# Two-head attention stage of a decoder: transposing the byte weights on TensorE instead of by DMA, with a rearranged schedule around it

## The chip, the core and the metric

The kernel runs on one core of a Trainium2 chip. A core has five engines with queues of their own: TensorE (PE, matrix multiplication into PSUM, with its weight loads as PEld), VectorE (DVE), ScalarE (ACT), GpSimd (POOL) and SyncE (SP, which here only issues DMAs). [...] Each engine works its queue in order: an instruction that waits holds up everything behind it. The metric is the device time of one execution in microseconds; lower is better.

## The reference

The program is a two-layer decoder over 2048 tokens of width 256. In each layer come an attention block, a cross-attention to a context of 2048 rows, and an MLP (a mixture of experts in the second layer), each followed by a layer norm. The change lies in layer 0, in the cross-attention and the MLP behind it:

```
q = fq_sym((x @ Wq + bq) / sqrt(16))          # 16 heads of 16, rounded to 8 bits per row
k = fq_sym(kv[..., 0]); v = fq_sym(kv[..., 1], axis=keys)
attn = softmax(q @ k.T)                       # 2048 queries x 2048 keys per head
attn = fq_unsigned(attn, axis=-1)             # rounded to 0..255 of the row's maximum
x = layernorm(x + (attn @ v) @ Wp + bp)
x = layernorm(x + (silu(gate) * up) @ w_down) # gate, up = x @ w_gate_up, inner width 1024
```

Since the weights are rounded to 256 steps of the row's maximum, the kernel computes exp(s - max + ln 255) straight into bytes.

## The kernel before

Cross-attention and MLP of layer 0 run as one "joint stage". The 2048 queries are 16 tiles of 128, taken as 8 pairs; a pair is 16 **steps**, (pair gp, head pair i, tile u), 128 steps in all. A step handles 2 heads x 128 queries x 2048 keys, and is issued in two **periods** (part 0 and 1), each over 1024 keys.

For step n, in order of the pipeline:

- `scores` (line 767): four bf16 matmuls a period on TensorE, 64 rows deep, so that head 0 and head 1 lie in different halves of the array. They write two PSUM tiles s, one a head, 4 KB per partition (two of the eight banks). Three such tiles exist; the rest of PSUM is one bank for the contexts (o) and one for everything else (misc).
- `scaled` (774): VectorE multiplies by the query's scale out of PSUM into e, and takes the row maximum on the way; two a period, one for each head. The second half's maximum includes that of the first.
- `exponent` (786): ScalarE makes the bias from the maxima at the end of the step.
- `weights8` (795): one step later, ScalarE writes exp as bytes a (128 queries x 2048 keys), head 0 in period 0, head 1 in period 1. Straight after it SP issues a DMA transpose (803) of a, seen as 128 x 1024 16-bit words, into at.
- `spread` (807): two steps after the scores, GpSimd takes the bytes of at apart (two to a word) and casts them to bf16 as aT, keys on the partitions.
- `context` (817): three to five steps after the scores, TensorE multiplies aT by the values, 16 matmuls for each pair of steps: 6 in period 1 of even steps, 5 in each period of odd steps.

The keys' order in the value tile (`values_by_key`, before the stage) matches the order in which the bytes come apart.

Between these, `pair_work` hands out pieces of other work by the step's number r in its pair and the period: queries for the next pair, whose quantised rows are transposed by DMA (`query_cols`, 612), division, output projection and layer norm of the pair before, and the MLP. An MLP unit is one of 8 slices of the inner width, in two halves `ffn_half` (gate and up, line 889, two f32 matmuls each), then tanh, copy and an affine step on ScalarE (907, 908, 911) and two products on GpSimd (914, 915). The units ran one per step at r = 8 to 15, and the down projection (924) at r = 1 to 3 of the next pair. TensorE's f32 matmuls each show as two records in the trace; its f32 transposes as one.

The order on all engines is written by hand (`manual_schedule`): what the loop emits is what the queues hold, and `later`/`due` put a piece off to a named period and place ("DVE", "ACT first", "ACT", "POOL", "SP" and so on). After the last step, up to 9 more steps drain the pipeline, and the last pair's MLP follows.

Of the kernel before, what the change touches and what calls it, by code (L numbers as in the profile page):

```python
# [20 lines left out]
U8 = mybir.dt.uint8  # L21
# [27 lines left out]
def decoder(ctx: ExitStack, tc: tile.TileContext, w: dict, out: bass.AP):  # L49
# [79 lines left out]

    pair_mv = {}  # L130

# [6 lines left out]

    def norm_pair(q):
        mv = pair_mv.pop(q)  # L140
        rstd = stat.tile([P, 2], F32, tag="np_rstd", name="np_rstd")
        nc.gpsimd.tensor_scalar(rstd, mv[:, :, 1], 1.0, 1e-5, ALU.mult, ALU.add)
        nc.gpsimd.tensor_tensor(rstd, rstd, mhalf, ALU.pow)
        shift = stat.tile([P, 2], F32, tag="np_shift", name="np_shift")
        nc.gpsimd.tensor_scalar(shift, mv[:, :, 0], -1.0, 0.0, ALU.mult, ALU.add)
        nc.gpsimd.tensor_tensor(shift, shift, rstd, ALU.mult)
        for i in range(2):
            x = xs[2 * q + i]
            nc.gpsimd.tensor_scalar(x, x, rstd[:, i : i + 1], shift[:, i : i + 1], ALU.mult, ALU.add)
# [420 lines left out]
    with ExitStack() as ph:  # L570
# [39 lines left out]

        def query_cols(t):
            nc.sync.dma_start_transpose(out=qT[t % 4].bitcast(U16), in_=rows3.rearrange("p h d -> p (h d)").bitcast(U16))

        qs = {}
        with tc.tile_pool(name="l0x_1", bufs=1) as p1, tc.tile_pool(name="l0x_p0", bufs=2, space=PSUM) as ps0:
# [35 lines left out]
            def values_by_key(t4):  # L651
                pt = ps0.tile([P, 4, 2, P], BF16, tag="pt3", name="ptv")
                for i in range(4):
                    for c in range(2):
                        at = t4 * G + (i // 2) * 2 * P
                        keys = vqT[:, c, at : at + 2 * P].rearrange("p (w j) -> p j w", j=2)
                        nc.tensor.transpose(pt[:, i, c, :], keys[:, i % 2, :], ident16)
                nc.scalar.copy(vq[:, 4 * t4 : 4 * t4 + 4, :].rearrange("p t (c d) -> p t c d", c=2), pt)
# [49 lines left out]
            for n in range(NB + 4):  # L708

                if n < NG:  # L710
                    values_of(n)
                if n < NB:
                    key_scale(n)
                for stage, f in ((1, key_steps), (2, key_round), (3, key_parts), (4, key_cols)):
                    if 0 <= n - stage < NB:
                        f(n - stage)
                if n == 3:
                    nc.vector.memset(rows3, 0.0)
                if n in (5, 8):
                    t = n // 8  # L720
                    a = query_max(t, query_proj(t, ps0, "pk"), p1)
                    query_scale(t)
                    query_round(a, query_inverse(t))
                if n in (7, 10):
                    query_cols(n // 10)
                if n == 4:
                    value_scale()
                if n in (6, 9, 12, 15):
                    quantise_values(n // 3 - 2)
                if n in (7, 10, 13, 16):  # L730
                    values_by_key(n // 3 - 2)
# [27 lines left out]
        def scores(gp, i, u, half, st):  # L759

            t = 2 * gp + u
            s = [ps.tile([P, 2, G], F32, tag="s", name="s", bufs=3) for _ in range(2)]
            for c in range(2):
# [24 lines left out]
        def weights8(gp, i, u, hh, st):  # L788
# [4 lines left out]

            a = wk.tile([P, 2 * G], U16, tag="a", name="a", bufs=3)
            nc.scalar.activation(  # L795
# [5 lines left out]
            )  # L801
            at = wk.tile([P, 8, P], U16, tag="at", name="at", bufs=4)
            nc.sync.dma_start_transpose(out=at, in_=a)
            st["at"].append(at)

        def spread(u, hh, st, aT):
            nc.gpsimd.tensor_copy(  # L807
                aT[:, :, hh, u * P : (u + 1) * P].rearrange("p (b j) q -> p b j q", j=2),
                st["at"][hh].bitcast(U8).rearrange("p b (q j) -> p b j q", j=2),
            )  # L810
# [70 lines left out]
        def ffn_gate(q, i, n, tag="misc"):  # L881

            if n == 0:
                pp = ps.tile([P, 2, G] if tag == "s" else [P, 2, 2 * P], F32, tag=tag, name="gu", bufs=3 if tag == "s" else 1)
                ffn_ps[q] = pp[:, 0].rearrange("p (n c) -> p n c", n=2) if tag == "s" else pp
# [23 lines left out]

        def ffn_sigmoid(th):  # L910
            nc.scalar.activation(th, th, AF.Copy, bias=0.5, scale=0.5)

# [4 lines left out]
        def ffn_down_psum(tag="misc"):  # L917
            pp = ps.tile([P, 2, G] if tag == "s" else [P, G], F32, tag=tag, name="pd", bufs=3 if tag == "s" else 1)
            return (pp[:, 0] if tag == "s" else pp).rearrange("p (u d) -> p u d", u=2)
# [29 lines left out]
        def query(t, at):  # L949
# [13 lines left out]
            later(at + 4, "POOL", lambda: query_round(box["a"], box["r"]))  # L963
            later(at + 5, "SP", query_cols, t)

# [7 lines left out]
        def put_out(gp, js, at):  # L973
# [7 lines left out]
            if 7 in js:  # L981
                later(at + 1, "POOL", norm_pair, gp)

        def ffn_half(q, i, n, at):
# [3 lines left out]
            if n == 1:  # L988
                th, gu = ffn_tiles(q, i)
                later(at, "ACT", ffn_out, q, th, gu)  # L990
                later(at + 1, "ACT", ffn_sigmoid, th)
                later(at + 2, "POOL", ffn_mult, q, i, th, gu, nc.gpsimd)
# [3 lines left out]
        def ffn_put_out(q, js, at, tag="misc"):  # L996
# [7 lines left out]
            if 2 * NI - 1 in js:  # L1004
                later(at + 1, "POOL", norm_pair, q)

# [6 lines left out]
        def by_dim(gp, u):  # L1013
            rbs[gp, u] = sums_by_dim(gp, u)

        def pair_work(n, end):

            gp, r = n // 16, n % 16
            at = 2 * n + end
            turn = (r, end)  # L1020
            if gp < LAST and turn in ((0, 0), (4, 0)):
                query(2 * gp + 2 + r // 4, at)

            if gp > 0:
                if turn == (4, 1):
                    divided(gp - 1, at)
                elif turn in ((5, 1), (6, 0), (6, 1)):
                    j = 3 * (2 * r + end - 11)
                    put_out(gp - 1, range(j, min(j + 3, 8)), at)
                elif turn == (7, 1):  # L1030
                    transposed(gp - 1, at)
                if turn in ((6, 0), (6, 1), (7, 0)):
                    ffn_load(2 * r + end - 12)
                if r >= 8 and not end:
                    ffn_half(gp - 1, r - 8, 0, at)

            if gp > 1:
                if (1, 0) <= turn <= (3, 1):
                    j = (0, 3, 6, 8, 11, 14, 16)[2 * r + end - 2 :]
                    ffn_put_out(gp - 2, range(j[0], j[1]), at)  # L1040
                elif turn == (5, 0):
                    transposed(gp - 2, at)

        def tail_work(n, end):
# [3 lines left out]
            turn = (r, end)  # L1048
            if turn in ((1, 0), (1, 1), (4, 0)):
                j = {(1, 0): (0, 4), (1, 1): (4, 8), (4, 0): (8, 16)}[turn]  # L1050
                ffn_put_out(LAST - 1, range(*j), at, "s")
# [11 lines left out]
        turns = {(7, 0): (0, 3), (7, 1): (3, 6), (8, 0): (6, 8), (8, 1): (8, 11), (9, 0): (11, 13), (9, 1): (13, 16)}  # L1063
        ordered = [getattr(mybir.EngineType, nm) for nm in ("PE", "DVE", "Activation", "Pool", "SP")]
        with tc.manual_schedule(engines=set(ordered)):
            for n in range(len(steps) + 9):
                now = steps[n] if n < len(steps) else None
                if now is not None:
                    if n % 16 == 0:
                        group(n // 16)  # L1070
                    if n < NB:
# [3 lines left out]
                        "mx": stat.tile([P, 2, 2], F32, tag="smx", name="smx"),  # L1075
                        "at": [],
                    }
                for part in range(2):
                    at = 2 * n + part
                    if now is not None:  # L1080
                        s = scores(*now, part, states[n])
                        scaled(*now, part, 0, states[n], s)
                        due(at, "DVE")
                        scaled(*now, part, 1, states[n], s)
                    else:
                        due(at, "DVE")
                    gp, r = n // 16, n % 16
                    if part == 1 and 0 < gp <= LAST and r >= 8:
                        ffn_half(gp - 1, r - 8, 1, at)
                    for hh in range(2):  # L1090
# [28 lines left out]
                    if 0 <= n - 2 < len(steps):  # L1119
                        gp, i, u = steps[n - 2]  # L1120
                        if part == 0 and u == 0:
                            aTs[gp, i] = wk.tile([P, NB, 2, 2 * P], BF16, tag="aT", name="aT")
                        spread(u, part, states[n - 2], aTs[gp, i])
                    due(at, "POOL")
                    if now is not None and part == 1:
                        exponent(states[n])
                    due(at, "DVE last")
                    due(at, "SP")
                    if (n, part) == (len(steps), 1):
# [7 lines left out]
                if n == len(steps) + 3:  # L1137
                    ffn_load_all()
                states.pop(n - 2, None)
            assert not put_off, put_off  # L1140

            for i in range(NI):
# [3 lines left out]
                ffn_out(LAST, th, gu)  # L1146
                ffn_sigmoid(th)
                ffn_mult(LAST, i, th, gu, nc.vector)
            exp_tables()
            for u in range(2):  # L1150
                ffn_put_out(LAST, range(NI * u, NI * u + NI), 0, "s")
                due(1, "DVE")
            due(1, "POOL")

    early_stage.close()
# [496 lines left out]
```

## Time and profile before

| | us |
|---|---|
| median of 3 runs | 2724.48 (2720.74 to 2729.77) |
| the profiled execution | 2727.17 |
| its span | 2725.2 |
| first to last start of the scaling, line 774 (the joint stage) | 880.4 to 1613.8 |
| byte casts on GpSimd, line 807, first to last start | 892.6 to 1626.4 |
| one DMA transpose of at on SP's queue, median | 1.23 |

| busy share of the span | PE | PEld | DVE | ACT | POOL |
|---|---|---|---|---|---|
| whole program | 92% | 55% | 70% | 54% | 45% |

In rows of groups, the fields are: line, engine, operation, written and read tiles, shapes and count; then total busy us and mean ns of one; then the engine's idle time just before the group and what ended it. In rows of the timeline: start us, duration, engine, line, operation, tiles, and in brackets the idle time before and its releaser. A row of waits gives the waiting engine and tile, whom it waited for, total us, times, longest. Durations are those of records, and on VectorE and ScalarE one record's end overlaps the next one's start by about 0.1 us, so the distance from start to start is the cost in a row of work. The whole-program shares mix stages with different limits; only the stretch from 880 to 1620 us concerns this change.

### The profile page before, as it was taken

The page shows a single profiled execution, that of the slowest core. Times are in us where ns is not written, and L with a number is a line of the kernel's source. Part 1 is how long each engine was busy: PE and PEld are TensorE (multiplying, and loading weights), DVE is VectorE, ACT ScalarE, POOL GpSimd, SP SyncE. Part 2 cuts the span into 40 slices and gives each one's busy share as a digit, 9 for nine tenths or more (in the row PEclk, how much of TensorE's full clock was granted, in tenths as well). Part 3 has the DMA queues.
Part 4 walks back from the last instruction along what each step waited for, and adds up shares of the span by engine and source line. Part 5 has one row for each costly group of instructions (what it writes and reads, how often), then busy time and mean ns, then how long its engine had stood idle before and what let it go on. Part 6 is the DMA issues. An engine that isn't in the chain of part 4 may idle for free. (4 is left out here: it accounts for less than half of the span.)

```text
span 2725.2 us, 39543 instructions
## 1 busy us (share of the span) xinstructions
PE 2519.4 (92%) x13877; PEld 1494.7 (55%) x13908; DVE 1903.5 (70%) x4365; ACT 1472.8 (54%) x2778; POOL 1215.8 (45%) x1336
## 2 busy tenths in 40 slices
PE   6999999999997788988988898999988899999998
PEld 3677777777764123433433345666655546564746
DVE  5677777877757999989999973777777742324232
ACT  3455555555543888977987873555554531313120
POOL 5544544444436888878888883223132200000000
PEclk9999999999998799999999999999999999999999
DMA  8000000000010566665665563100100011112120
GB/s 252 1 1 1 1 1 1 1 1 1 1 39 13 103 111 119 128 111 115 124 124 107 112 141 94 59 2 2 44 15 11 2 66 43 54 39 61 33 67 10
DMA packets 360150, 150.69 MB, mean 55 GB/s; under 512 B 294576, under 2 KB 341136, under 8 KB 359440
## 3 DMA queue, kind: packets, MB, share of 16 engines
q1 hardware_dynamic: 358592, 144.49, 22.9%
q0 software_dynamic: 1360, 3.68, 0.6%
q8 instruction: 110, 1.80, 0.3%
q14 instruction: 88, 0.72, 0.1%
HBM read 74.57 MB, written 2.23 MB: 28 GB/s over the span
## 5 line engine op out<-in xcount | busy, mean ns | idle before, releaser
L807 POOL CAST aT<-at 128x2048 bf16<-128x2048 uint8 x256 | 481.2, 1894 | 88.9 <-DMA at<-a 83.0
L795 ACT ACTIVATE a<-e,snl 128x2048 uint8<-128x2048 f32 x256 | 510.8, 1996 | 3.5
L774 DVE TENSOR_SCALAR_CACHE_REDUCE e<-s,qs,smx 128x1024 f32<-128x1024 f32 x256 | 335.2, 1335 | 14.7 <-PE s L767 13.9
L774 DVE TENSOR_SCALAR_CACHE_REDUCE e<-s,qs 128x1024 f32<-128x1024 f32 x256 | 319.9, 1281 | 33.8 <-PE s L767 28.8
L817 PE MATMUL o<-aT,vq 128*32 128x512 bf16 x1024 | 266.3, 395 | 3.3 <-POOL aT L807 3.3
L767 PE MATMUL s<-kT,qT 64*128 64x512 bf16 x1024 | 189.8, 399 | 30.0 <-DVE e L774 27.1
L1564 DVE TENSOR_TENSOR h<-h,up 128x512 f32<-128x512 f32 (+1 forms) x100 | 68.8, 688 | 192.4 <-PE up L1560 191.0
L1563 ACT ACTIVATE h<-gate 128x512 f32<-128x512 f32 (+1 forms) x100 | 59.7, 597 | 220.5 <-PE gate L1560 220.2
L817 PEld LDWEIGHTS <-vq 128*32 128x32 bf16 x1024 | 86.2, 98 | 165.5 <-issue 91.8
L1560 PE MATMUL gate<-xT,w_L_ffn_w1g 128*128 128x512 f32 x352 | 167.7, 595 | 0.0
L1560 PE MATMUL up<-xT,w_L_ffn_w1u 128*128 128x512 f32 x352 | 165.4, 592 | 0.0
L1274 DVE TENSOR_REDUCE amx<-sc 128x8 f32<-128x1024 f32 x96 | 116.7, 1216 | 62.4 <-PE sc L1265 62.2
L1591 PE MATMUL py<-w_L_ffn_w2T,h 128*128 128x256 f32 x704 | 154.6, 379 | 0.0
L1277 ACT ACTIVATE pr<-pr 128x1024 f32<-128x1024 f32 x96 | 101.6, 1059 | 88.3 <-DVE pr L1276 88.3
L1286 ACT COPY prT<-tp 128x512 f32<-128x512 f32 x192 | 104.3, 584 | 76.9 <-PE tp L1285 76.5
L1591 PEld LDWEIGHTS py<-w_L_ffn_w2T,h 128*128 128x128 f32 x704 | 133.7, 190 | 18.3
L889 PE MATMUL gu<-xT,wgu 128*128 128x256 f32 x448 | 132.3, 419 | 9.6 <-ACT gu_s L908 4.9
L425 ACT ACTIVATE pls<-sc,lm,rms_rs 128x128 f32<-128x128 f32 x256 | 113.8, 454 | 21.7 <-DVE lm L421 21.7
L355 PE MATMUL proj<-Wlk,xT 128*128 128x512 f32 x256 | 121.5, 597 | 3.0 <-ACT raw_Wlv L381 1.8
L482 PE MATMUL po<-Wo,mT 128*128 128x256 f32 x512 | 121.2, 380 | 1.4 <-ACT mT L474 1.4
L355 PE MATMUL proj<-Wq,xT 128*128 128x512 f32 x256 | 122.3, 601 | 0.2 <-DVE raw_Wlk L364 0.2
L1276 DVE TENSOR_TENSOR pr<-sc,amx 128x1024 f32<-128x1024 f32 x96 | 117.0, 1219 | 5.7
(313 smaller groups left out, 5383.5 us busy)
## 6 DMA issues: line engine op xcount, KB each, us to landing
wgu<-in_L_ffn_gu SPq DMA_DIRECT2D x112, 128.0 KB
sh<-share SPq DMA_DIRECT2D x32, 256.0 KB
at<-a SPq DMA_TRANSPOSE x256
sh<-share SPq DMA_DIRECT2D x16, 224.0 KB
sh<-share SPq DMA_DIRECT2D x16, 192.0 KB
w_L_ffn_w1g<-in_L_ffn_w1g SPq DMA_DIRECT2D x1, 2816.0 KB
w_L_ffn_w1u<-in_L_ffn_w1u SPq DMA_DIRECT2D x1, 2816.0 KB
w_L_ffn_w2T<-in_L_ffn_w2T SPq DMA_DIRECT2D x1, 2816.0 KB
```

Source lines behind the costliest of these rows:

```text
L355: nc.tensor.matmul(pp.rearrange("p h d -> p (h d)"), lhsT=xTt(b, k), rhs=wts[nm, hg][:, k, :], start=k == 0, stop=k == 1)
L482: nc.tensor.matmul(outs[b], lhsT=st["mT"][:, h, :], rhs=wts["Wo", hg][:, h, :], start=hg == 0 and h == 0, stop=hg == 3 and h == 3,)
L767: nc.tensor.matmul(s[hh][:, c, :], lhsT=qT[t % 4][r, i, :], rhs=kT[r, i, at : at + G], start=True, stop=True)
L774: nc.vector.tensor_scalar(st["e"][hh][:, half, :], s[hh].rearrange("p a b -> p (a b)"), qs[2 * gp + u][:, 2 * i + hh : 2 * i + hh + 1], No ...
L795: nc.scalar.activation(a.bitcast(U8), st["e"][hh].rearrange("p a b -> p (a b)"), AF.Exp, bias=st["nm"][:, hh : hh + 1], accum_out=groups[g ...
L807: nc.gpsimd.tensor_copy(aT[:, :, hh, u * P : (u + 1) * P].rearrange("p (b j) q -> p b j q", j=2), st["at"][hh].bitcast(U8).rearrange("p b ...
L817: nc.tensor.matmul(o[r : r + 32].rearrange("p a b -> p (a b)"), lhsT=vq[:, n, 32 * i : 32 * i + 32], rhs=aT[:, n].rearrange("p a b -> p (a ...
L889: nc.tensor.matmul(ffn_ps[q][:, n, :], lhsT=wt[:, k, :], rhs=xT[q // 2][:, k, at], start=k == 0, stop=k == 1)
L1274: nc.vector.tensor_reduce(mx, sc, AX.X, ALU.max)
L1276: nc.vector.tensor_tensor(pr, sc, bc(mx, 2, P), ALU.subtract)
L1560: nc.tensor.matmul(pp[:rows], lhsT=wt[:, k, :], rhs=xT[g][:, k, :], start=k == 0, stop=k == 1)
L1591: nc.tensor.matmul(py, lhsT=h[:rows, i4 * P : (i4 + 1) * P], rhs=wt, start=n == 0, stop=n == len(parts) - 1)
```

## The change

- The bytes of a are now seen as 128 x 512 words of 32 bits. `words_T`: TensorE transposes them, four 128 x 128 transposes, into one PSUM bank (tag tp, two buffers). `words_out`: the result is copied to at as 1024 16-bit words a partition, by VectorE for head 1 (in period 0, of step n - 2) and by ScalarE for head 0 (in period 1, of step n - 1). a has four buffers, at three.
- To make room in PSUM, the score tiles s have two buffers in place of three.
- In VectorE's queue the put-off work now follows both scalings and is followed by the copy, where before it stood between the scalings. In TensorE's queue the word transposes come right after the scores. In ScalarE's queue the copy comes before the period's exponential.
- `spread` takes four bytes out of a word in place of two, and `values_by_key` orders the values to match.
- The query columns are transposed by TensorE and copied by ScalarE; two DMA transposes before the stage and 14 in it go.
- The affine step of an MLP unit is on GpSimd (in the tail on VectorE). The 8 units run at r = 9, 11, 12, 14, 15 and then 0, 1, 2 of the next pair; the down projection moves to r = 3 to 5, and division, output projection, transposes of x and queries move too. `norm_pair` is cut in two put-off pieces on GpSimd.
- SP is no longer in the hand-written order.

```diff
-        def query_cols(t):
-            nc.sync.dma_start_transpose(out=qT[t % 4].bitcast(U16), in_=rows3.rearrange("p h d -> p (h d)").bitcast(U16))
+        def query_cols(psum, tag):
+            pt = psum.tile([P, 8, P], BF16, tag=tag, name="ptq", bufs=2)
+            for i in range(8):
+                nc.tensor.transpose(pt[:, i, :], rows3[:, 2 * i : 2 * i + 2, :].rearrange("p h d -> p (h d)"), ident16)
+            return pt
...
-            s = [ps.tile([P, 2, G], F32, tag="s", name="s", bufs=3) for _ in range(2)]
+            s = [ps.tile([P, 2, G], F32, tag="s", name="s", bufs=2) for _ in range(2)]
...
-            a = wk.tile([P, 2 * G], U16, tag="a", name="a", bufs=3)
+            a = wk.tile([P, G], F32, tag="a", name="a", bufs=4)
...
-            at = wk.tile([P, 8, P], U16, tag="at", name="at", bufs=4)
-            nc.sync.dma_start_transpose(out=at, in_=a)
-            st["at"].append(at)
+            st["a"].append(a)
+
+        def words_T(hh, st):
+            pt = ps.tile([P, 4, P], F32, tag="tp", name="aTp", bufs=2)
+            for b in range(4):
+                nc.tensor.transpose(pt[:, b, :], st["a"][hh][:, b * P : (b + 1) * P], ident)
+            return pt
+
+        def words_out(hh, st, pt, copy):
+
+            at = wk.tile([P, 4, P], F32, tag="at", name="at", bufs=3)
+            copy(at.bitcast(U16), pt.bitcast(U16))
+            st["at"][hh] = at
 
         def spread(u, hh, st, aT):
             nc.gpsimd.tensor_copy(
-                aT[:, :, hh, u * P : (u + 1) * P].rearrange("p (b j) q -> p b j q", j=2),
-                st["at"][hh].bitcast(U8).rearrange("p b (q j) -> p b j q", j=2),
+                aT[:, :, hh, u * P : (u + 1) * P].rearrange("p (b j) q -> p b j q", j=4),
+                st["at"].pop(hh).bitcast(U8).rearrange("p b (q j) -> p b j q", j=4),
             )
...
-        def ffn_sigmoid(th):
-            nc.scalar.activation(th, th, AF.Copy, bias=0.5, scale=0.5)
+        def ffn_sigmoid(th, eng):
+            eng.tensor_scalar(th, th, 0.5, 0.5, ALU.mult, ALU.add)
...
-            later(at + 5, "SP", query_cols, t)
+            later(at + 5, "PE", lambda: box.update(T=query_cols(ps, "tp")))
+            later(at + 6, "ACT first", lambda: nc.scalar.copy(qT[t % 4], box["T"]))
...
-                later(at + 1, "POOL", norm_pair, gp)
+                later(at + 1, "POOL", norm_pair_scale, gp)
+                later(at + 2, "POOL first", norm_pair_rows, gp)
...
+        units = {9: 0, 11: 1, 12: 2, 14: 3, 15: 4, 0: 5, 1: 6, 2: 7}
+
+        def unit(n, k, at):
+
+            gp, r = n // 16, n % 16
+            q = gp - 1 if r >= 8 else gp - 2
+            if r in units and 0 <= q < LAST:
+                ffn_half(q, units[r], k, at)
...
-                        scaled(*now, part, 0, states[n], s)
-                        due(at, "DVE")
-                        scaled(*now, part, 1, states[n], s)
-                    else:
-                        due(at, "DVE")
-                    gp, r = n // 16, n % 16
-                    if part == 1 and 0 < gp <= LAST and r >= 8:
-                        ffn_half(gp - 1, r - 8, 1, at)
+                        for hh in range(2):
+                            scaled(*now, part, hh, states[n], s)
+                    due(at, "DVE")
+
+                    m = n - 2 + part
+                    if 0 <= m < len(steps):
+                        pt = words_T(1 - part, states[m])
+                        words_out(1 - part, states[m], pt, nc.scalar.copy if part else nc.vector.tensor_copy)
+                    due(at, "PE")
+                    if part == 1:
+                        unit(n, 1, at)
```

## The prediction

> **What bounds the kernel now.** I read the page first, then the stage alone by windows, then one steady step of the timeline, then the waits. The page's costliest rows are four instructions of the joint stage, each 256 times: one step (two heads of 128 queries against 2048 keys) has two of each.
>
> ```profile
> L807 POOL CAST aT<-at 128x2048 bf16<-128x2048 uint8 x256 | 481.2, 1894 | 88.9 <-DMA at<-a 83.0
> L795 ACT ACTIVATE a<-e,snl 128x2048 uint8<-128x2048 f32 x256 | 510.8, 1996 | 3.5
> L774 DVE TENSOR_SCALAR_CACHE_REDUCE e<-s,qs,smx 128x1024 f32<-128x1024 f32 x256 | 335.2, 1335 | 14.7 <-PE s L767 13.9
> L774 DVE TENSOR_SCALAR_CACHE_REDUCE e<-s,qs 128x1024 f32<-128x1024 f32 x256 | 319.9, 1281 | 33.8 <-PE s L767 28.8
> ```
>
> The reader sees that VectorE hardly waits for anything, and that GpSimd's 83 us of waiting for the DMA transposes is idle time of an engine with time to spare. The first scaling starts at 880.4 us and the last at 1613.8 us: (1613.8 - 880.4 - 1.2) / 127 = 5.76 us a step, 128 steps. The stage's middle by engine (columns: stretch, length, then busy us with instruction counts for PE, PEld, DVE, ACT, POOL, then granted clock, DMA share, GB/s):
>
> ```profile
> 1000.00:1400.00 400.00, 360.29 (x1644) 156.59 (x1644) 372.51 (x631) 338.99 (x460) 340.86 (x299) 0.97 0.61 119
> ```
>
> VectorE is busy 93% (5.36 us of a step), TensorE 90% (5.19, at a clock of 0.97), GpSimd 85% (4.91), ScalarE 85% (4.88). VectorE is the bound, with 0.40 us a step to spare. The waits say who follows whom:
>
> ```profile
> ACT snl L786 <- DVE e L774: 53.2, 38, 3.0
> ACT xT L160 <- PE ln_pt L155: 3.8, 4, 1.5
> ACT th L907 <- PE gu L889: 2.2, 2, 1.2
> ```
>
> 53 of ScalarE's 61 idle us (69 steps) are one wait: the row maxima of the step. So ScalarE has about 0.8 us a step to spare, as long as it waits for VectorE alone. One step of its queue:
>
> ```profile
> 1060.91 0.29 ACT L786 ACTIVATE snl<-smx,ln 128x2 f32<-128x2 f32 x1 [0.94 <-DVE e L774]
> 1061.24 2.00 ACT L795 ACTIVATE a<-e,snl 128x2048 uint8<-128x2048 f32 x1
> 1063.15 0.19 ACT L795 ACTIVATION_READ_ACCUMULATOR a<-e,snl 128x1 f32 x1
> 1063.24 1.99 ACT L795 ACTIVATE a<-e,snl 128x2048 uint8<-128x2048 f32 x1
> 1065.13 0.19 ACT L795 ACTIVATION_READ_ACCUMULATOR a<-e,snl 128x1 f32 x1
> 1065.93 0.29 ACT L786 ACTIVATE snl<-smx,ln 128x2 f32<-128x2 f32 x1 [0.61 <-DVE e L774]
> ```
>
> The two exponentials run back to back.
>
> **What is removed.** 256 DMA transposes and the wait of GpSimd for them. No engine that sets the pace waits for GpSimd here (TensorE's wait for aT is 3.3 us in the whole stage), so I count nothing for it. If the few waits of VectorE for s that GpSimd could cause all went, at most its 0.40 us a step would come back.
>
> **VectorE: a copy a step.** It copies head 1's transposed words, 128x1024 of 16 bits out of PSUM. The trace has no 16-bit VectorE read of PSUM. The nearest row by elements is the scaling itself: 1024 elements out of PSUM, one start to the next 1.20 us. The Trainium skill (VectorE: DVE Perf Modes, the perf-mode tier table) lets a copy out of PSUM take two elements a cycle when everything is 16-bit and contiguous, never more; its 120 + 512 cycles at 0.96 GHz make 0.66 us, an estimate. A row of 512 elements out of PSUM (raw_Wlk, line 364) has 0.68 us. I take the rule, and 0.60 us start to start (the rows overlap their successor by about 0.08): 0.60 x 128 = +77 us of VectorE work; by the scaling's row it would be 1.2 x 128 = +154. This cannot hide: 0.60 is above the 0.40 spare. New busy time 5.96 us.
>
> **VectorE: two score buffers in place of three.** Score matmuls go out as (keys 0, head 0), (0, head 1), (1, head 0), (1, head 1). With three buffers the next period's second matmul needs the buffer of head 0, free since 1.2 us. With two it needs head 1's, which VectorE reads until the period's end; head 0 is complete only with the third matmul. So at each edge VectorE waits for a hand-over, matmuls two and three (0.4 to 0.6; four together take 0.61 in the timeline) and 0.13 back (matmuls end 1065.94, the scaling starts 1066.07): 0.5 to 0.7 us. In the first period of a step its word copy fills that; in the second only the small operations do, which now come after both scalings. I charge 0.5 a step: VectorE's own loop becomes 6.46 us.
>
> **TensorE.** Eight f32 transposes a step. Rows: four of the same shape (pt_r, line 839) take 0.60 us, eight (tp, line 1285) 1.04, so 0.11 each in a row: +0.88, less in than out; busy 5.19 + 0.88 = 6.07. The skill (TensorE: Matmul & The Clock Gate, Part 4) says that the clock gate does not count transposes as work. If that halved the clock for them, 0.88 more a step, +113 us. From 2000 to 2180 us, where 216 records of such transposes run, the granted clock is 0.97: I take no loss.
>
> **ScalarE: a copy, and a wait between the exponentials.** This step decides. In the second period the copy of head 0's words stands in ScalarE's queue before head 1's exponential, and what it copies was written by head 0's exponential, the instruction just before it. So ScalarE must hand to TensorE, wait for four transposes, and go on. Behind the waiting copy stand head 1's exponential and the next step's bias; GpSimd's spreads, and VectorE's and TensorE's next pieces, wait for those. Its loop from the rows: bias 0.33 (1060.91 to 1061.24); exponential with its accumulator read 2.10 (to 1063.34); transposes 0.60 plus 0.04 each way (the gap of snl after VectorE) 0.68; copy of 1024 halfwords 1.01 (line 706, the same shape out of PSUM: 1012 ns); second exponential 2.10; an MLP unit's tanh and copy every second step, 0.73 / 2 = 0.37; the rest (ot and xT copies, two each, and two new query copies per 16 steps) 0.27. Sum 6.86. The other way, from busy time: 4.88 - 0.20 (the affine step, 402 ns each second step, gone) + 1.01 + 0.13 (query copies) + 0.68 = 6.50. I take the middle, 6.65: a floor that holds if TensorE is always ready.
>
> It is not. Between a step's two transpose groups TensorE's queue has, in odd steps, five contexts (1.25), a half MLP unit or a piece of the down or output projection (1.13 to 1.56) and the scores (0.43 before something can follow). That is 2.8 to 3.2 us after the first group of 0.6, while head 0's exponential is ready 2.4 us after the last one (3.2 where a tanh and copy lie between). So head 0's transposes start 0 to 1.2 us late in odd steps, about on time in even ones: 0.3 on the mean, and 0.05 for VectorE's edge. **Step: 6.65 + 0.35 = 7.0 us.**
>
> **At nothing, with their cover.** The affine step on GpSimd: 0.41 us each second step on an engine at 4.91 that, without the 0.6 of DMA wait, stays below 5.2 of 7.0; uncovered 0.20 x 128 = 26. Spread by words of four: the same 2048 elements in runs of 128, so 1.89 us stays. Moved MLP units, normalisations and queries: the same instructions and weight loads, spread elsewhere; GpSimd's two half-norms cost nothing while it has slack. The query columns: 14 DMA transposes in the stage become 8 bf16 transposes (0.61, line 705) and a copy each, counted above; the two early ones, about 1 us either way. SP leaves the hand-written order and has only weight loads left there. In the tail the last transposes shorten (the DMA kept GpSimd waiting from 1624.2 + 1.9 to 1626.4), and three MLP units of the last pair but one slip into it: -3 to +4, taken as 0.
>
> **Sum.** (7.0 - 5.76) x 128 = +159 us. The profiled execution took 2727.2 us, of which 2725.2 is the span; so 2886 for it. The median of the runs is 2.7 lower: **2884 us**.
>
> **Rivals.**
> (1) *VectorE or TensorE sets the pace.* The word copy goes at one element a cycle: 5.36 + 1.2 + 0.5 = 7.06 alone, and with the coupling just worked out 7.5 to 7.8; 2724.5 + 128 x 1.9 = 2968. For it: no 16-bit read of PSUM in the trace. Against: rule and pattern fit.
> (2) *Only VectorE's addition counts*, ScalarE's wait falling into the 0.8 us it has: 5.96 + the idle of today 0.40 = 6.36, +77, 2801. For it: ScalarE idles now. Against: that idle is before the bias, the new wait is between exponentials, and 1.01 + 0.68 exceeds 0.86 anyhow.
> (3) *Faster.* One mechanism: freed from the DMA's delay, VectorE's idle goes and its copy hides in it. At best 0.40 x 128 = 51 us, 2673. It decides only where copy plus edge stay under 0.40 us a step; the copy alone would have to run above twice the rate of the rule.
> (4) *No change*: gains and costs cancel, 2724; it needs the same point exactly.
>
> **How the numbers follow.** The main case 0.62 (its own range 2835 to 2945: the floor of 6.50 plus little, to a coupling of 0.85); rival 1, 0.18; rival 2, 0.14; rival 3, 0.04; rival 4, 0.02. A measurement of this kernel tells some 0.3% from no change (the three runs span 0.33%). Faster 0.04, same 0.02, slower 0.94. The range leaves out the faster cases, half of rival 2 and a third of rival 1: 2800 to 2980.
>
> **What would show it.** In the profile after: steps of about 7.0 us by the first and last start of the scaling; a new wait of ScalarE's at copy for TensorE's transposes, some 0.7 us or more in every step, and the exponentials no longer back to back; the at copy near 0.66 us on VectorE and 1.0 on ScalarE; VectorE's wait for s up from 22 us in 400; busy share of VectorE down to about 85%; DMA share near 0.1 in place of 0.61; the spread still 1.89 us. It is wrong if the step lies under 6.5 us (ScalarE's copy was not in its chain, or TensorE's transposes came before it was needed), or over 7.6 (a 1.2 us copy, a halved clock, or a queue that blocks across engines worse than one group at a time).

## The result, and the profile after

The change makes the kernel slower: 2940.19 us median against 2722.89 for the kernel before in the same session, a ratio of 1.0793 (95% interval 1.0773 to 1.0813). The forecast of 2884 had the direction, and its range of 2800 to 2980 holds the result; the loss was 217 us where the sum said 159.

The profiled execution's span is 2938.4 us against 2725.2, 213.2 more. The joint stage took 202.8 of that: from the first start of a scaling (880.0) to the last one in a step's first period (1816.2) it is 936.2 us, before 733.4. (1816.2 and the 1613.8 of before are these starts; the very last scalings, in the last step's second period, start at 1819.9 and 1616.5.) From 1816.2 to the next stage's first projection it is 71.6 us against 63.2, another 8.4, and the rest of the program takes 1050.6 against 1048.1. A step is (1816.2 - 880.0 - 1.2) / 127 = 7.36 us, from 5.76.

The costliest groups of the page after, in the form of those shown of before:

```profile
L823 POOL CAST aT<-at 128x2048 bf16<-128x2048 uint8 x256 | 482.5, 1891 | 246.1 <-DVE at L819 205.7
L801 ACT ACTIVATE a<-e,snl 128x2048 uint8<-128x2048 f32 x256 | 513.4, 2006 | 2.8
L780 DVE TENSOR_SCALAR_CACHE_REDUCE e<-s,qs 128x1024 f32<-128x1024 f32 x256 | 318.5, 1282 | 137.6 <-PE s L773 113.2
L780 DVE TENSOR_SCALAR_CACHE_REDUCE e<-s,qs,smx 128x1024 f32<-128x1024 f32 x256 | 333.6, 1341 | 34.2 <-PE s L773 33.7
...
L773 PE MATMUL s<-kT,qT 64*128 64x512 bf16 x1024 | 198.9, 392 | 51.6 <-DVE e L780 50.1
L819 ACT COPY at<-aTp 128x1024 uint16<-128x1024 uint16 x128 | 129.5, 1012 | 200.6 <-PE aTp L813 185.7
```

The cast, the exponential and the scalings take what they took before, within 0.5%. What has grown is waiting in a circle: VectorE 147 us for the scores (43 before), TensorE 50 us for VectorE to free a score tile (27 before), ScalarE 186 us for the transposed words. The busy share of every engine has fallen (same columns as in the stretch shown of before):

```profile
1000.00:1400.00 400.00, 346.62 (x1738) 168.28 (x1737) 325.82 (x544) 313.62 (x390) 273.99 (x248) 0.97 0.06 17
```

VectorE fell from 93% to 81%, TensorE from 90% to 87%, ScalarE from 85% to 78%. On the mean, none is as full as VectorE was. Of the largest waits from 1050 to 1550 us, some 68 steps:

```profile
ACT at L819 <- PE aTp L813: 100.0, 63, 3.9
POOL aT L823 <- DVE at L819: 98.1, 58, 4.5
DVE e L780 <- PE s L773: 75.7, 86, 2.1
...
PEld aTp L813 <- ACT a L801: 62.7, 80, 1.7
```

ScalarE's queue in one step shows the wait that the forecast was built on, between the two exponentials:

```profile
1208.16 0.21 ACT L801 ACTIVATION_READ_ACCUMULATOR a<-e,snl 128x1 f32 x1
1209.17 1.01 ACT L819 COPY at<-aTp 128x1024 uint16<-128x1024 uint16 x1 [0.80 <-PE aTp L813]
1210.08 2.00 ACT L801 ACTIVATE a<-e,snl 128x2048 uint8<-128x2048 f32 x1
```

So far the profile looks like the forecast's main case, only larger. The experiments show that this holds only in part.

### The profile page after: what moved, and what is told of

The parts are those of the page before. It is cut to its first block, busy times and chain, and to the rows that moved or that the text cites. A ratio compares the mean times of both kernels' runs of the same rounds, so it can differ in the third digit from the quotient of the medians.

```text
span 2938.4 us, 41659 instructions
## 1 busy us (share of the span) xinstructions
PE 2689.9 (92%) x15060; PEld 1616.9 (55%) x15060; DVE 1988.6 (68%) x4501; ACT 1586.6 (54%) x2858; POOL 1237.4 (42%) x1392
## 5 line engine op out<-in xcount | busy, mean ns | idle before, releaser
L823 POOL CAST aT<-at 128x2048 bf16<-128x2048 uint8 x256 | 482.5, 1891 | 246.1 <-DVE at L819 205.7
L801 ACT ACTIVATE a<-e,snl 128x2048 uint8<-128x2048 f32 x256 | 513.4, 2006 | 2.8
L780 DVE TENSOR_SCALAR_CACHE_REDUCE e<-s,qs 128x1024 f32<-128x1024 f32 x256 | 318.5, 1282 | 137.6 <-PE s L773 113.2
L780 DVE TENSOR_SCALAR_CACHE_REDUCE e<-s,qs,smx 128x1024 f32<-128x1024 f32 x256 | 333.6, 1341 | 34.2 <-PE s L773 33.7
L773 PE MATMUL s<-kT,qT 64*128 64x512 bf16 x1024 | 198.9, 392 | 51.6 <-DVE e L780 50.1
L819 ACT COPY at<-aTp 128x1024 uint16<-128x1024 uint16 x128 | 129.5, 1012 | 200.6 <-PE aTp L813 185.7
L813 PE MATMUL aTp<-ident,a 128*128 128x128 f32 x1024 | 177.5, 298 | 54.6 <-ACT a L801 53.9
L813 PEld LDWEIGHTS aTp<-ident,a 128*128 128x128 f32 x1024 | 113.3, 147 | 176.3 <-ACT a L801 135.8
L773 PEld LDWEIGHTS <-qT 64*128 64x128 bf16 x1024 | 41.2, 94 | 167.5 <-issue 166.1
```

Of the source, the lines that this page charges most:

```text
L773: nc.tensor.matmul(s[hh][:, c, :], lhsT=qT[t % 4][r, i, :], rhs=kT[r, i, at : at + G], start=True, stop=True)
L780: nc.vector.tensor_scalar(st["e"][hh][:, half, :], s[hh].rearrange("p a b -> p (a b)"), qs[2 * gp + u][:, 2 * i + hh : 2 * i + hh + 1], No ...
L801: nc.scalar.activation(a.bitcast(U8), st["e"][hh].rearrange("p a b -> p (a b)"), AF.Exp, bias=st["nm"][:, hh : hh + 1], accum_out=groups[g ...
L813: nc.tensor.transpose(pt[:, b, :], st["a"][hh][:, b * P : (b + 1) * P], ident)
L819: copy(at.bitcast(U16), pt.bitcast(U16))
L823: nc.gpsimd.tensor_copy(aT[:, :, hh, u * P : (u + 1) * P].rearrange("p (b j) q -> p b j q", j=4), st["at"].pop(hh).bitcast(U8).rearrange(" ...
```

## The experiments

Two names used below: **quiet steps** are r = 0 to 2 and 9 to 15 of a pair, **projection steps** are r = 3 to 8, where the down projection, the division and the output projection now lie. All step times are the distances between the first scalings of successive steps in the traces, means over pairs 2 to 6. The "first pair" is the 16 steps of pair 0, in which there is no MLP and no output projection yet. Steps are numbered by r. The granted clock is that of TensorE. The kernel before took 2723 to 2728 us in the four sets of runs; differences of a few us between sets say nothing.

### ScalarE's copy moved behind the exponential

```diff
-                        words_out(1 - part, states[m], pt, nc.scalar.copy if part else nc.vector.tensor_copy)
+                        if part == 0:
+                            words_out(1, states[m], pt, nc.vector.tensor_copy)
...
                         weights8(*steps[n - 1], part, states[n - 1])
+                    if part == 1 and 0 <= m < len(steps):
+                        words_out(0, states[m], pt, nc.scalar.copy)
```

> Only ScalarE's word copy moves: in the second period it comes after head 1's exponential, not before it. Nothing else changes; TensorE still transposes head 0's words in the same place and waits there for head 0's exponential. Theory S (ScalarE's chain with the wait between its exponentials sets the step of 7.36 us): 1.6 us of wait a step go from the chain, the step falls to 6.5 to 6.8, where VectorE (5.96 busy plus the edge) takes over: 2830 to 2870 us. Theory V (VectorE's copy and the two score buffers set it already): no change, 2930 to 2950. Theory Q (TensorE's queue, blocked at the transposes until the exponential is done, sets it): little, 2910 to 2945.

Measured: 2908.91 us, ratio 1.0669 (1.0653 to 1.0685): 31 us better than the change. ScalarE's wait for the words, in the same 500 us, falls from 100 us to

```profile
ACT at L819 <- PE aTp L813: 34.5, 29, 3.0
```

and yet quiet steps go only from 7.06 to 6.78 us, projection steps from 8.19 to 8.08. ScalarE's chain was real, but when it goes another one stands right behind it. In steps 1, 9 and 11 that is TensorE's own queue: they take 6.54 us each, and TensorE works through them without a gap. Step 9 of pair 3, columns as in the stretches above:

```profile
1285.93:1292.47 6.54, 6.54 (x35) 3.15 (x34) 5.72 (x10) 6.27 (x9) 4.83 (x4) 1.00 0.14 40
```

In the change itself step 9 already takes 6.54 us, with TensorE busy for 6.53. Theory S in its strong form falls.

### All word work one period later

```diff
-                    m = n - 2 + part
+                    m = n - 2
...
-                        pt = words_T(1 - part, states[m])
-                        words_out(1 - part, states[m], pt, nc.scalar.copy if part else nc.vector.tensor_copy)
+                        pt = words_T(part, states[m])
+                        words_out(part, states[m], pt, nc.vector.tensor_copy if part else nc.scalar.copy)
```

(the casts one period later as well)

> Word transposes, copies and casts all run one period later, so that every transposed byte tile was finished a whole period before: head 0 in the first period with ScalarE's copy, head 1 in the second with VectorE's. The same instructions in all. Theory S: both ScalarE's wait between exponentials and TensorE's wait for them go; the step is VectorE's, 6.4 to 6.7 us: 2815 to 2855 us. Theory V: 2920 to 2950. Theory Q: as far below the run that moves the copy alone as TensorE's blocking is worth, at 1.28 us a step of TensorE's waits for the byte tiles some 50 us or more; theory S expects 0 to 25 us between the two.

Measured: 2932.64 us, 1.0757 (1.0741 to 1.0773), 8 us better than the change. TensorE's wait for the byte tiles is nearly gone (its weight loads wait 8.9 us for them in the same 500 us, from 62.7), ScalarE's for the words is not: 85.2 us. In this order the copy waits for transposes that stand behind scores, and those wait for VectorE. Taking away TensorE's blocking on ScalarE gained little here; since ScalarE's wait stayed, the run does not price the blocking alone, and why this order is 24 us worse than the one before it was not settled.

### Both copies on VectorE

```diff
-                        words_out(1 - part, states[m], pt, nc.scalar.copy if part else nc.vector.tensor_copy)
+                        words_out(1 - part, states[m], pt, nc.vector.tensor_copy)
```

> VectorE copies the words of both heads, each where the change has a copy; ScalarE copies none. Theory S: ScalarE's exponentials run back to back again, VectorE's work grows by 0.60 us a step to 6.56 and both edges of a step are covered by a copy: a step of 6.8 to 7.1, 2865 to 2905 us, faster than the change although its busiest engine has more to do. Theory V: 0.60 us more a step on the engine that sets the pace: 3000 to 3020.

Measured: 2921.51 us, 1.0715 (1.0697 to 1.0733): outside both bands. VectorE has 0.60 us more to do in each step, and the time still falls by 19 us, so VectorE's amount of work is not what sets the step. The shortest steps are 6.54 us here and in the run with ScalarE's copy moved, although VectorE copies once there and twice here: these are TensorE's, and the second copy falls into a hole that VectorE had anyway. The next run shows where such holes come from.

### Two score buffers alone

```diff
-            s = [ps.tile([P, 2, G], F32, tag="s", name="s", bufs=3) for _ in range(2)]
+            s = [ps.tile([P, 2, G], F32, tag="s", name="s", bufs=2) for _ in range(2)]
```

(in the kernel before; the two other tiles that share these buffers likewise)

> The kernel before with the score tiles cut from three buffers to two, and nothing else. By the edge worked out in the prediction (0.5 to 0.7 us at each of two edges a step, with 0.4 us of idle there is already): a step of 6.3 to 6.6 us, 2790 to 2830 us. If two buffers are enough: 2720 to 2730, and the edge is no part of the loss.

Measured: 2855.49 us, 1.0474 (1.0458 to 1.0489). This one number is 130 us, 60% of the change's loss, and more than was expected of it. The timeline of that run at the end of a period:

```profile
1204.36 0.09 DVE L774 DVE_READ_ACCUMULATOR e<-s,qs 128x1 f32 x1
1204.49 0.59 PE L767 MATMUL s<-kT,qT 64*128 64x512 bf16 x3 [0.83 <-DVE e L774]
1204.93 1.34 DVE L774 TENSOR_SCALAR_CACHE_REDUCE e<-s,qs,smx 128x1024 f32<-128x1024 f32 x1 [0.48 <-PE s L767]
```

VectorE finishes at 1204.45; only then can the other three score matmuls of the next period go, and VectorE starts again at 1204.93. In the steps without projections (9 to 15 in this order) this happens at both edges: 6.18 to 6.27 us, which is the scalings' 2 x (1.205 + 1.27) = 4.95 plus two gaps of 0.62 to 0.66. Steps 8 to 15 cost 0.73 us more than before on the mean, steps 0 to 7, with the projections, 1.15 more. TensorE also waits, 0.83 us here. My reading is that with two buffers it cannot run ahead, and whatever makes one engine late in a period is lost for both. In the stage VectorE's wait for scores is 168 us, from 43, and TensorE's for VectorE 127, from 27. A lower clock goes with it: over the stage 0.93 is granted, 0.95 before. Counted as (1 - clock) x length, that is some 23 us more lost TensorE time, an estimate; whether it adds to the 130 us or only follows from the waiting was not isolated.

In the first pair, with little beside the attention, the 16 steps take 85.5 us before, 106.1 with two buffers, and 107.9 with the change. There the transposes, the copies and the new order together add 1.8 us out of 22.4; all else comes with the missing buffer.

### The new order without its transposes

The change's order with DMA transposes for words and query columns and three score buffers; then the same with two.

```diff
...
+            at = wk.tile([P, 8, P], U16, tag="at", name="at", bufs=4)
+            nc.sync.dma_start_transpose(out=at, in_=a)
...
-                    m = n - 2 + part
-                    if 0 <= m < len(steps):
-                        pt = words_T(1 - part, states[m])
-                        words_out(1 - part, states[m], pt, nc.scalar.copy if part else nc.vector.tensor_copy)
...
```

> The change's order of work (MLP units over two pairs, moved pieces, affine step on GpSimd, small VectorE work after both scalings) with the transposes of before: DMA for words and query columns, three score buffers, SP in the hand-written order. If the new order by itself costs nothing: 2715 to 2735 us. If it adds to the loss (its tail took 8 us more, and small work at a period's end no longer lies between the scalings): 2735 to 2790. Faster than before by at most VectorE's idle, 2690, if spreading the MLP fills holes.

> The same with two score buffers: the change without its transposes on TensorE and without the copies. Two buffers alone cost the kernel before 130 us. Theory L (with two buffers TensorE cannot run ahead, so each period takes the longer of VectorE's and TensorE's work in it, and evenly spread work suffers less): 2800 to 2850, below the 2855 of two buffers alone, since the MLP is spread over more periods. Plain sum of the two parts: 2855 plus what the new order costs alone.

Measured: 2800.43 us with three buffers (1.0271, 1.0251 to 1.0291) and 2873.05 with two (1.0537, 1.0519 to 1.0555); the first is above all that was expected. The order alone costs 74 us, and one buffer less on top of it 73, against 130 by itself. The two overlap; both lengthen VectorE's wait for scores (103 us with the order alone, 168 with both, 43 before). What the transposes and copies add to the last of these is 2940 - 2873 = 67 us; 31 of it go when ScalarE's copy moves, and no run takes the rest apart. The first pair is faster in the new order with three buffers, 82.0 us; the loss lies in steps 3 to 11, most of it in the projection steps (up to 10.8 us a step). The expectation that even spreading would soften two buffers failed: 2873 is above 2855.

### Scores by head

```diff
-            for c in range(2):
-                at = (2 * half + c) * G
-                for hh in range(2):
-                    r = slice(64 * hh, 64 * hh + 64)
+            for hh in range(2):
+                r = slice(64 * hh, 64 * hh + 64)
+                for c in range(2):
+                    at = (2 * half + c) * G
```

> The change with its score matmuls by head: both of head 0, then both of head 1. Head 0's tile can then be refilled while VectorE still scales head 1, so the hand-over at the edge of a period leaves VectorE's path; but the pairs in different halves of the array no longer run side by side, 0.43 us more for TensorE in each period. Theory E (the exposed hand-over is what two buffers cost): faster, 2830 to 2890. Theory L (TensorE's work in a period, now longer, is what counts): the same or slower, 2935 to 3010.

Measured: 2938.08 us, 1.0773 (1.0754 to 1.0793), no difference from the change. The earlier hand-over does work where TensorE has little else to do: the stage's first step takes 4.95 us in place of 6.52. But step 4 of the same pair takes 8.86 in place of 7.31, and in pairs 2 to 6 nothing is left of the gain (quiet steps 7.07, projection steps 8.24). What takes it back, the lost pairing or something else, this run does not tell.

### Half of the gate and up matmuls

```diff
-            for k in range(2):
+            for k in range(1):
```

> The change with the second half of the inner sum of the gate and up products left out (wrong MLP, the same tiles, copies and waits): two of an MLP unit's four f32 products of 128x128x256, 0.9 us of TensorE each unit, 0.45 us a step; outside the stage the last pair's tail loses about 7 us as well. Theory L: TensorE's work in a period counts in more than half of the periods, the stage gives back 25 to 50 us and the time is 2880 to 2910. Theory S or V (ScalarE's chain or VectorE sets the step, TensorE has spare time): only the tail's 7, 2925 to 2935.

Measured: 2936.48 us, 1.0769 (1.0744 to 1.0793). TensorE loses 0.45 us of work a step, and the time nothing beyond what the tail was to give: the tail is 5.4 us shorter, the stage 1.3 longer. From this alone one would say that TensorE's work sets nothing. The steps say otherwise. Steps 9, 11 and 14 fall by 0.33 to 0.37 us, to 6.21 to 6.32, about what the hand-overs alone take (6.18 to 6.27 above), and step 1 from 6.96 to 6.35. The gain is lost again elsewhere, most of all in step 0, which goes from 7.36 to 8.64. Steps 9 and 0 of pair 3, first the change and then this run:

```profile
1296.15:1302.69 6.54, 6.53 (x34) 3.07 (x32) 5.72 (x9) 4.71 (x5) 4.34 (x4) 1.00 0.14 40
1296.93:1303.14 6.21, 6.19 (x30) 2.39 (x28) 5.63 (x10) 4.53 (x5) 4.56 (x4) 1.00 0.16 42
...
1225.59:1232.95 7.36, 6.08 (x30) 2.90 (x30) 5.63 (x10) 6.56 (x9) 5.84 (x6) 1.00 0.13 39
1225.28:1234.23 8.95, 7.02 (x28) 2.66 (x29) 5.63 (x10) 8.12 (x15) 7.25 (x7) 0.81 0.10 30
```

TensorE still counts as busy in the shorter step 9 because a score matmul that waits for VectorE is counted too: the first four take 0.94 us there, 0.60 in the change. In step 0 the granted clock is 0.81 in place of 1.00, and a context matmul takes up to 0.63 us in place of 0.38. So theory L is right for single quiet steps, and a lower clock goes along with the loss that hides it in the sum; what lowers the clock was not tested. (The projections were untouched in this run.)

### Where VectorE's small work stands

In projection steps the profile after shows this at the end of a period (TensorE and VectorE):

```profile
1379.08 1.34 DVE L780 TENSOR_SCALAR_CACHE_REDUCE e<-s,qs,smx 128x1024 f32<-128x1024 f32 x1
...
1380.35 0.42 DVE L873 TENSOR_TENSOR x<-x,pd 128x256 f32<-128x256 f32 x1
...
1380.82 1.56 PE L940 MATMUL pd<-w_L_ffn_d,h 128*128 128x256 f32 x6 [0.89 <-DVE x L873]
...
1382.31 0.60 PE L773 MATMUL s<-kT,qT 64*128 64x512 bf16 x4
...
1383.05 1.28 DVE L780 TENSOR_SCALAR_CACHE_REDUCE e<-s,qs 128x1024 f32<-128x1024 f32 x1 [1.61 <-PE s L773]
```

The next piece of the down projection needs the add's read of the same PSUM tile to be over. The add now comes after both scalings, the piece after the add, the next scores after the piece, and VectorE idles 1.6 us. Three runs move the small work and nothing else, each in another kernel; the edit is

```diff
-                        for hh in range(2):
-                            scaled(*now, part, hh, states[n], s)
-                    due(at, "DVE")
+                        scaled(*now, part, 0, states[n], s)
+                        due(at, "DVE")
+                        scaled(*now, part, 1, states[n], s)
```

in the change (first), in the new order with DMA and three buffers (second), and the reverse of it in the kernel before (third):

> The change with VectorE's put-off work (adds to x, statistics, division, query maxima) back between the two scalings of a period, as it was before; all else as changed. Theory B (in steps 3 to 8 of a pair, pieces of the down and output projection on TensorE wait for an add on VectorE that now comes after both scalings; the next scores stand behind them, and VectorE idles): the add comes 1.2 to 1.3 us earlier and a scaling covers TensorE, 0.5 to 1.3 us in each of some 5 steps a pair, 25 to 55 us in all: 2885 to 2915. Theory S alone (ScalarE's copy) or the cover that the prediction credited to small work at a period's end: 2935 to 2960.

> The new order with DMA transposes and three score buffers (2800 us) and VectorE's put-off work back between the scalings. Theory B: most of its 74 us of loss goes, 2725 to 2765; below 2715 if the other moves help, since its first pair, which has no projections, took 82.0 us against 85.5 before. If the loss comes from the other moves (down projection behind GpSimd's last product, division and projections next to each other): 2780 to 2800.

> The kernel before with one thing changed: VectorE's put-off work after both scalings of a period. Theory B: TensorE's pieces of the projections wait until the period's end, then the scores stand behind them: 2750 to 2790 us. If the place of the small work does not matter: 2720 to 2730.

Measured: 2967.42 us (1.0877, 1.0861 to 1.0893), 2743.21 us (1.0053, 1.0038 to 1.0068) and 2778.64 us (1.0187, 1.0172 to 1.0202). With three buffers small work at the period's end costs 50 us (third against before) or 57 (first form of the new order against the second). Adds of this kind then hold TensorE for up to 3.0 us (1.8 before); the kernel before with that one edit, from 1050 to 1550 us:

```profile
PE pq L584 <- DVE x L857: 15.1, 5, 3.0
...
PE py L852 <- DVE x L857: 10.4, 5, 2.1
PE pd L924 <- DVE x L857: 10.4, 5, 2.1
```

With two buffers the sign turns: putting it back between the scalings costs 27 us. The steps show that theory B holds there too, but is outweighed. In steps 4 and 7, which have the adds, the time falls as it says (8.25 to 7.29 and 8.67 to 7.89); step 6 goes from 7.65 to 10.73 and step 8 from 7.98 to 9.51. In step 6 the small work is the division's product of 1.22 us. Between the scalings it puts off the second one, whose end frees the tile that the next scores need:

```profile
1281.17 1.22 DVE L862 TENSOR_TENSOR ot<-ot,pt_r 128x1024 f32<-128x1024 f32 x1
...
1282.31 1.28 DVE L780 TENSOR_SCALAR_CACHE_REDUCE e<-s,qs 128x1024 f32<-128x1024 f32 x1
...
1283.64 1.01 PE L773 MATMUL s<-kT,qT 64*128 64x512 bf16 x3 [1.96 <-DVE e L780]
```

The clock falls as well; the same step 6 of pair 3, in the change and in this run:

```profile
1272.13:1279.47 7.34, 5.62 (x29) 2.67 (x27) 6.76 (x10) 5.06 (x7) 6.65 (x8) 1.00 0.00 0
1279.96:1289.88 9.92, 7.26 (x31) 3.43 (x31) 6.85 (x10) 5.94 (x7) 6.53 (x5) 0.83 0.00 0
```

How much of the 27 us is the later scaling and how much the clock, no run isolates. That the change has the better place of the two for its two buffers is measured; that the small work at a period's end fills the hand-over there, as the forecast had it, is argued.

### Copy moved and small work between

The edits of the first experiment and of the last, together.

> The change with both: ScalarE's word copy after head 1's exponential (31 us by itself) and VectorE's put-off work between the scalings. If the two causes lie in different steps of a pair, as the step times show (the copy in steps 0 to 3, 12 and 15; the adds in 3 to 8), the gains add: 2855 to 2885. If one hides the other: near the better of the two alone. In no case under 2800: two score buffers and VectorE's copy hold every step above 6.2 us.

Measured: 2933.59 us, 1.0753 (1.0735 to 1.0771), outside what was expected, since one of the two was no gain. The parts add, with their measured signs: 2967 less 34, where the copy alone was worth 31.

A ladder from one kernel to the other, each rung one run against the last:

| | us | step up | granted clock over the stage |
|---|---|---|---|
| kernel before | 2723 to 2728 | | 0.95 |
| new order, DMA, three buffers, small work between | 2743 | +15 to +20 | 0.96 |
| small work after both scalings | 2800 | +57 | 0.93 |
| two score buffers | 2873 | +73 | 0.92 |
| transposes on TensorE, copies (the change) | 2940 | +67 | 0.95 |

The price of a rung depends on the rungs below it, as 73 against 130 for the buffer shows. The clock moves along with them, and a rung's price includes whatever the clock did. None of the versions run is faster than the kernel before.

## Why the prediction came out as it did

**The bound and the sizes of the parts.** The durations held: VectorE's word copy 688 ns (0.66 by the Trainium skill, VectorE: DVE Perf Modes, the cycle table of its section on the TRN2 errata with the tier table's two elements a cycle; the trace agrees within 5%), ScalarE's copy 1012, four transposes 0.66 where 0.60 was taken, the cast 1.89, the clock of the stretch 0.97. The rivals on a slow copy and a halved clock fell with that. VectorE at 81% was less than the 85% forecast, the DMA share 0.06 where 0.1 was written.

VectorE as *the* bound was a mean. Step by step two engines alternated before. Steps 9 and 10 of pair 3:

```profile
1206.25:1211.81 5.56, 5.56 (x27) 2.48 (x26) 5.11 (x8) 3.94 (x8) 3.92 (x4) 1.00 0.48 108
1211.81:1216.88 5.07, 4.97 (x23) 2.06 (x23) 5.03 (x9) 5.04 (x8) 4.26 (x4) 1.00 0.61 106
```

In step 9, with ten contexts, TensorE is busy all the time and VectorE is not; in step 10, with six, VectorE is the fuller of two that are nearly full. The forecast gave TensorE its mean of 6.07 us and dropped it from the maximum. In step 9 its work is 6.53 after the change, and that is the step.

**"This step decides": ScalarE's wait.** The wait is there, 0.80 us at its shortest where the sum had 0.68, and 1.6 a step on the mean (200.6 us of idle before 128 copies, 185.7 of it put down to the transposes) where the sum had about 1.0. Taking it away gave 31 us, where a fall from the forecast's 7.0 to VectorE's loop of 6.46 would have been 69. What stood behind it was not that loop in every step, but in some of them TensorE's queue with 6.54. Naming ScalarE as the one that decides was too much. (The middle of its two sums, 6.86 and 6.50, is 6.68 and not 6.65: 4 us in all.)

**"Two score buffers in place of three".** Each edge was sized right: 0.5 to 0.7, measured 0.62 to 0.66. What failed is the charge of "0.5 a step", inside VectorE's loop only, so that in a maximum with ScalarE's it vanished. Alone the buffer is worth 130 us, 1.0 us a step, more than any other part measured alone, and more in steps with projections than in the others (1.15 against 0.73). A gap per edge does not give that difference; that the third buffer was the room in which TensorE ran ahead over uneven periods fits it, but no run shows it alone.

**"At nothing": the moved work.** The missing 58 us lie for the most part in the projection steps. They take 8.19 us; at six such steps in some 6.5 pairs, 1.19 above the forecast of 7.0 is 46 us. The forecast spread one step time over all 128 steps, put moved MLP units, projections and small work at zero, and did not ask who waits for the adds. With three buffers the moves cost 74 us in all, 57 of them by the place of the small work. With two they cost 2873 - 2855 = 18, and the steps with projections are long in the old order too (7.41 us in steps 0 to 7 with two buffers alone). So how much of the 46 us is moved work and how much the missing buffer stays open.

**How far the number was luck.** Quiet steps came to 7.06 us, close to the 7.0 forecast for every step. But that is a mean of steps from 6.54 to 7.93 set by different engines, not one loop of ScalarE's with a delay. A wait that weighed less than said and a buffer that weighed more pull the sum in opposite ways. Direction, durations and the new wait were understood; that the total came inside the range was luck in part.

**The tail.** Taken as 0 (-3 to +4), measured +8.4. The new order with DMA transposes has 67.8 us there against 63.2, so 4.6 of it come with the order; three MLP units and the down projection slipped behind the last scores in it, but no run isolates these.

**The rivals.** A slow VectorE copy: no. Only VectorE's addition (2801): no; ScalarE's copy, the buffer and the order each have a price. Faster, or no change: far from it. No rival named TensorE's queue in single steps, or the buffer as the largest part.

## What to carry to other kernels

A PSUM buffer taken away is priced by its own run, not as a gap in one engine's loop: here it was worth 130 us alone and 73 with the new order in place, against the 31 of the wait that looked decisive in the profile. When several loops lie within some per cent, the largest wait in the profile names one that bounds, not how much its removal gives; and a mean over a long stretch hides that the bound changes from step to step, so look at single steps too. A small operation put off in a queue has a price through whoever waits for it: moving it to the period's end was +50 us with three buffers and -27 with two. A run that changes nothing in total can still move single steps both ways.

## What was not expected of the hardware

VectorE reads 1024 halfwords from PSUM in 688 ns, ScalarE in 1012 for the same tile, so which engine copies is worth 0.3 us of engine time a tile. Eight f32 transposes a step on TensorE left its granted clock as it was: 0.97 in the stretch from 1000 to 1400 us and 0.95 over the stage, in both kernels. Edits that only changed the order or left work out went with a lower one in single steps: 0.81 in step 0 with half of the gate and up matmuls, 0.83 in step 6 with the small work between the scalings, both 1.00 in the change. And with the DMA share from 1000 to 1400 us down from 0.61 to 0.06 the compute instructions compared took as long as before: the scalings 1282 and 1341 ns in place of 1281 and 1335, the cast 1891 in place of 1894, the exponential 2006 in place of 1996. So these show no sign that the transposing DMAs had slowed them.
